# A sparse attention layer on one core: the late query rows are computed in natural order, and the sort of the late half is done a pair later

## The chip, the core and the metric

The kernel runs on one core of a Trainium2 chip. The time is that of one execution in device microseconds. A core has TensorE (PE) for matmuls, VectorE (DVE), ScalarE (ACT), GpSimd (POOL) and SyncE (SP); each works through its own instruction list in order, and SP, ACT and POOL also issue DMAs.

## The reference

`x` has 2708 rows of 1024 numbers, `adj` is a 2708 by 2708 matrix of zeros and ones in which a one stands with probability 0.0014771, so a row has four edges on average.

```python
h = relu(layernorm(x))
q = h @ W_q.T + b_q;  k = h @ W_k.T + b_k;  v = h @ W_v.T + b_v
z = (q @ k.T) / 32 * adj
attn = softmax(where(z == 0, -10000, z), axis=1)
out = x + relu(attn @ v)
```

## The kernel before, in words

**Products.** `W_q` and `W_k` are folded into one matrix M at the start, so that a score is a row of h times M times a row of h. What is called q in the code is h times M, and it is compared with rows of h directly. The result of attention is a weighted sum u of rows of h, and only after that it is multiplied by `W_v`. There are 21 full tiles of 128 rows and one tile of 20 rows. Two tiles at a time (a *unit*) are multiplied by M, and later by `W_v`, with seven block products instead of eight: `blocks` (L646) forms the sums s1 to s4 of the four half rows, `multiply` (L949) issues the seven products (`add_block`, L913, four matmuls of 128x512 each, two passes in the trace). Units 0 to 4 are the q of tiles 0 to 9, tile 10 goes alone at the end of unit 4 (`single_query`, L1131), units 5 to 9 are the q of tiles 11 to 20, units 10 to 19 are the outputs.

**Edges.** Each row of `adj` is searched for its ones: `found` (L330) runs four FIND_INDEX8 on DVE for a tile, `counted` (L324) sums the row on ACT, `listed` (L340) makes up to 16 neighbour numbers of a row, for four tiles at a time.

**Sort.** To gather no more neighbours than needed, the rows are sorted by their number of edges, in two parts: the early part (tiles 0 to 10, `EARLY = 11`) and the late part (the rest). `counts` (L596) makes on DVE a one-hot table `hot` of the counts, `sort` (L613) has two bf16 matmuls on PE (`ps_in` and `ps_all`, L619 and L621) count over it, and seven DVE instructions turn them into the place of each row. `put` (L568) scatters an entry of the table for each row (its neighbours, its number, its count) to DRAM by that place, `reload` (L580) reads the table back in sorted order.

**q and the order of rows.** The early tiles get q in natural order into `q_dram`; attention then gathers a sorted tile's q rows by their number. The late tiles get q in sorted order: their h rows are gathered by the reloaded table (`first_rows`, L556, and `load_rows`, L1095), the result lies in `q_late` in sorted order, and attention reads it with a plain DMA (`fetch`, L760). The rows that sort to the end, the last 20, have no edges and need no q.

**Attention** (`attention`, L859) runs on DVE, ACT and POOL beside the products: for a sorted tile it gathers one row of h for each slot (`fill`, L773), a DVE instruction (L794) multiplies it with q and sums it up to the score, an exponential on ACT and some small DVE instructions make the weights, and DVE sums the weighted rows (L847). `K` says how many slots a sorted tile has.

**What sets the order.** The first stage (until unit 5) has the order of DVE, ACT and POOL written out by hand. `after(i)` (L1162) is called at seven points of each unit n, and `steps_at` (L704) names the search steps at (n, i): `f20` is found and listed for tile 20, `i15` and `j15` are found and listed apart, `p` is counted, `c` is `counts` and `o` is `sort` of the early part, `w` its `put` and `reload`. In unit 3 the late part follows: `counts` at (3, 3), `sort` at (3, 4) with `issue_after`, then `entered` (L632): `put`, `reload`, the rows of units 5 and 6, and the last additions to the sum of all rows (`owe`). `searched` (L712) closes the buffers of the search and opens the gather slots, three of which POOL clears; `ts_of_wv` (L729) makes with 16 DVE instructions (L734 to L737) the sums of `W_v` blocks that SP stores to `tv_dram` (L739). From unit 5 on the scheduler orders POOL and ACT, and `advance` hands out the attention's steps between the products.

Of the kernel before, what the change touches and what calls it, by code (L numbers as in the profile page):

```python
# [18 lines left out]
P = 128  # L19
# [7 lines left out]
TW = 18  # L27
ROWS = 7
HIGH = 11
EMPTY = (10, 20)  # L30
EARLY = 11
# [27 lines left out]
def tile_preln_masked_attention(  # L59
# [76 lines left out]
    nc.vector.memset(zall, 1.0)  # L136
# [10 lines left out]
    rows_i = const.tile([P, NT], I32, name="rows_i")  # L147
    nc.gpsimd.iota(rows_i, pattern=[[P, NT]], base=0, channel_multiplier=1)
    nc.vector.memset(tab, 0.0)
    nc.vector.tensor_copy(tab.bitcast(U32)[:, :, SLOTS:SLOTS + 1], rows_i.unsqueeze(2))  # L150

# [3 lines left out]
    down_i = const.tile([P, ND], I32, name="down_i")  # L155
    nc.gpsimd.iota(down_i, pattern=[[-1, ND]], base=SLOTS, channel_multiplier=0)
    down = const.tile([P, ND], FT, name="down")
# [13 lines left out]
    first_i = const.tile([P, PARTS, 8], I32, name="first_i")  # L171
    nc.gpsimd.iota(first_i, pattern=[[-PW, PARTS], [0, 8]], base=N, channel_multiplier=0)
    first = const.tile([P, PARTS, 8], FT, name="first")
    nc.vector.tensor_copy(first, first_i)

# [17 lines left out]
    def stats(group):  # L193

        G = len(group)
        mv = stat.tile([P, 4, 2], FT, tag="mv", name="mv")
        if tiles[group[-1]][1] < P:
            nc.vector.memset(mv, 1.0)
        xs = []
        for i, t in enumerate(group):  # L200
            t0, n = tiles[t]
            if EARLY + 4 <= t < EARLY + 7:
# [189 lines left out]
    with tc.tile_pool(name="w", bufs=1, side="left") as wp:  # L392
# [136 lines left out]
        follow("f8")  # L529
# [24 lines left out]
    FIRST = EARLY // 2  # L554

    def first_rows(n):  # L556

        rows_of[FIRST + n] = [row_tile(f"qr_{t}") for t in (EARLY + 2 * n, EARLY + 2 * n + 1)]
        for k, row in enumerate(rows_of[FIRST + n]):
            last = gather(row, h_dram[:, :], EARLY + 2 * n + k, SLOTS, P)  # L560
        return last
# [34 lines left out]
    def counts(lo, hi):  # L596


        n = hi - lo
        s1, s2 = [work.tile([P, D], FT, tag="hT", name=name, bufs=2) for name in ("sort", "hot")]  # L600
        sorting[:] = s1, s2
        found = s1[:, 0:n * SLOTS].rearrange("p (t s) -> p t s", s=SLOTS)
        nc.vector.tensor_scalar(found, keys[:, lo:hi], 0.0, None, op0=ALU.is_gt)
        nc.vector.tensor_reduce(bad[:, lo:hi], found, AX.X, ALU.add)
        nc.vector.tensor_copy(tab[:, lo:hi, SLOTS + 1:SLOTS + 2], bad[:, lo:hi].unsqueeze(2))
        nc.vector.tensor_sub(deg[:, lo:hi], bad[:, lo:hi], past[:, lo:hi])
        nc.vector.tensor_scalar_max(deg[:, lo:hi], deg[:, lo:hi], -1.0)
        nc.vector.tensor_tensor(s2.bitcast(BF)[:, 0:ND * n].rearrange("p (d t) -> p d t", d=ND),
                                deg[:, lo:hi].unsqueeze(1).to_broadcast([P, ND, n]),
                                down.unsqueeze(2).to_broadcast([P, ND, n]), op=ALU.is_equal)  # L610
        nc.vector.tensor_scalar(tab.bitcast(U32)[:, lo:hi, 0:SLOTS], keys[:, lo:hi], -1.0, float(N), op0=ALU.mult, op1=ALU.add)

    def sort(lo, hi):  # L613

        s1, s2 = sorting
        W = ND * (hi - lo)
        hot = s2.bitcast(BF)[:, 0:W]
        ps_in = psum.tile([P, NB], FT, tag="tp", name="ps_in")
        nc.tensor.matmul(ps_in[:, :W], before, hot, start=True, stop=True)  # L619
# [3 lines left out]
        nc.vector.tensor_copy(cnt, ps_all[:, :W])  # L623
        run = s1[:, W:2 * W]
        nc.vector.tensor_tensor_scan(run, cnt, cnt, 0.0, op0=ALU.add, op1=ALU.max)
        nc.vector.tensor_sub(run, run, cnt)
        nc.vector.tensor_add(run, run, ps_in[:, :W])
        nc.vector.tensor_mul(run, run, hot)
        nc.vector.tensor_reduce(deg[:, lo:hi], run.rearrange("p (d t) -> p t d", d=ND), AX.X, ALU.add)
        return nc.vector.tensor_copy(pos_i[:, lo:hi], deg[:, lo:hi])  # L630

    def entered():  # L632

        with tc.issue_after(put(EARLY, NT).ins):
            late = reload(EARLY, NT)
        with tc.issue_after(late.ins):
            rows = first_rows(0)
        with tc.issue_after(rows.ins):
            rows = first_rows(1)
        with tc.issue_after(rows.ins):  # L640
            for t in sorted(owed):
                owe(t)
# [42 lines left out]
    def natural_rows(n):  # L685
# [4 lines left out]
    ops_of[0][1]()  # L690
    ops_of[0][2]()
# [20 lines left out]
    def searched():  # L712
        nc.vector.tensor_tensor(bad, bad, total, op=ALU.not_equal)
# [12 lines left out]
        assert len(adj_loads) == NT  # L726
        free.extend([M.rearrange("p i j (a c) w -> p i j a (c w)", a=2)[:, 0, 1, a, :] for a in range(2)] + slots[8:])
# [14 lines left out]

    wanted, g_of, tq, first_q = [], {}, {}, []
# [16 lines left out]
    def fetch(t):  # L760

        assert t in formed
# [3 lines left out]
        if t < EARLY:  # L766
            got = gather(tq[t], q_dram[:, :], t, SLOTS, P)
            if t == order[0]:
                first_q.append(got)
        else:  # L770
            nc.gpsimd.dma_start(tq[t], q_late[(t - EARLY) * P:(t - EARLY + 1) * P, :])

    def fill():  # L773
        while wanted and free:
            t, s = wanted.pop(0)
            g = free.pop(0)
            with tc.issue_after(first_q[0].ins) if first_q else nullcontext():
                gather(g, h_dram[:, :], t, s, P, skip=True)
# [79 lines left out]

    def attention(order):  # L859
# [5 lines left out]
        with tc.issue_after(chain[-1].ins):  # L865
            for lo, hi in parts:
                nc.vector.tensor_scalar(valid[:, lo:hi], ptab.bitcast(U32)[:, lo:hi, 0:SLOTS], float(N) - 0.5, NONE,
                                        op0=ALU.is_lt, op1=ALU.max)
        free.extend(slots[:8])
        fill()  # L870
        yield 0.0
        fetch(order[0])
# [19 lines left out]
    order = [8, 7, 6, 5, 4, 3, 2, 0, 1, 9, 15, 14, 13, 12, 16, 17, 20, 10, 18, 19, 11]  # L892
# [56 lines left out]
    def multiply(n, results, after):  # L949
# [22 lines left out]
        results[3](Y)  # L972
        if n == FIRST - 1:

            single_query()
            opened(n + 1)
        after(6)
# [112 lines left out]
    q_pairs = [(t, t + 1) for t in range(0, EARLY - 1, 2)] + [(t, t + 1) for t in range(EARLY, FULL, 2)]  # L1090
# [4 lines left out]
    def load_rows(unit):  # L1095
        kind, *pair = unit
        rows = []
        for t in pair:
# [4 lines left out]
            if kind == "q":  # L1103
                gather(rows[-1], h_dram[:, :], t, SLOTS, P)
# [19 lines left out]
    def single_turned(s):  # L1124

        if s == 0:
            single["row"] = kept.pop(EARLY - 1)
# [3 lines left out]
    def single_query():  # L1131
# [3 lines left out]
        dst = q_dram[(EARLY - 1) * P:, :]  # L1135
# [8 lines left out]
        ops_of[FIRST][2]()  # L1144
        rows_of.pop(FIRST)
        nc.sync.dma_start(dst[:, lo], q[:, lo])
        formed.add(EARLY - 1)
# [3 lines left out]
    for n, unit in enumerate(units):  # L1151
# [10 lines left out]
        def after(i):  # L1162
            if (n, i) in steps_ahead:
                follow(steps_ahead[n, i])
            if (n, i) == (3, 3):
                counts(EARLY, NT)
            if (n, i) == (3, 4):
                with tc.issue_after(products[-1].ins):
                    placed.append(sort(EARLY, NT))
                entered()  # L1170
            if (n, i) in ((4, 1), (4, 2)):
                ts_of_wv(2 * i - 2, 2 * i)
            if (n, i) == (FIRST - 1, 2):
                next(stream)
# [4 lines left out]
            if (n, i) >= (FIRST, 1):  # L1179
                advance(share)  # L1180
            if nxt is not None:
# [19 lines left out]
                if i == (2 if n == FIRST else 4) and n + 2 >= FIRST and n + 2 < len(units) and n + 2 not in rows_of:  # L1201
# [35 lines left out]
    with tc.issue_after(chain[-1].ins):  # L1237
# [10 lines left out]
        nc.vector.tensor_add(many, many, deg[:, 0:1])  # L1248
    ps_f = psum.tile([P, NB], FT, tag="tp", name="ps_f")
# [210 lines left out]
```

## Time and profile before

| | |
|---|---|
| median of 3 runs | 666.57 us (665.93 to 668.82) |
| the profiled execution | 668.54 us |
| its span, first to last instruction | 666.8 us |
| PE busy, share of the span | 653.1 us, 98% |
| DVE, ACT, POOL busy | 79%, 40%, 60% |
| mean granted TensorE clock | 0.993 |
| matmuls of L913 with x320 and 128x512 outputs | 593 to 598 ns from start to end of one |

The profiled execution is one of its own, 1.97 us above the median; around its span lie 1.7 us. PE's matmuls are pipelined, so they overlap: eight passes of a block take 3.43 us from start to start of the next block. "Idle before" in the profile is the time that an engine waited, with what ended the wait; PEclk is the clock that TensorE was granted, 1.00 being full speed.

### The profile page before, as it was taken

What the parts mean: (1) busy time and instruction counts of PE and PEld (TensorE: products, weight loads), DVE (VectorE), ACT (ScalarE), POOL (GpSimd) and SP (SyncE); (2) the same over time, 40 slices, a digit from 0 to 9 for tenths busy, and PEclk for the clock granted to TensorE, in tenths of its full rate; (3) what the DMA queues carried; (4) which work ended last, traced back from release to release, by engine and by line L of the source; (5) the groups of instructions that cost most, each with busy time, mean ns of one, the idle gap of its engine ahead of it and who ended that gap; (6) DMA issues with size and microseconds to landing.
All of it is one profiled execution on the core that took longest, in us unless ns stands there. A gap on an engine that the chain in (4) does not pass through costs nothing.

```text
span 666.8 us, 6383 instructions
## 1 busy us (share of the span) xinstructions
PE 653.1 (98%) x1770; PEld 333.5 (50%) x1770; DVE 528.1 (79%) x1014; ACT 263.6 (40%) x395; POOL 402.1 (60%) x398
## 2 busy tenths in 40 slices
PE   9999999999998999999999999999999999999994
PEld 5777765444443444444444444444444444445441
DVE  5997899979999404988887999798788998989221
ACT  3558975765843212332241231332332434323200
POOL 2559991666386763775556365574674878863331
PEclk9999999999998999999999999999999999999998
DMA  8995999699757796897889999998987899894631
GB/s 339 407 344 199 375 362 393 222 392 330 256 177 258 276 360 243 283 386 244 308 316 354 375 416 391 308 309 244 339 286 193 236 295 364 232 312 132 149 120 66
DMA packets 62164, 193.24 MB, mean 290 GB/s; under 512 B 9689, under 2 KB 10041, under 8 KB 61226
## 3 DMA queue, kind: packets, MB, share of 16 engines
q0 software_dynamic: 34464, 109.25, 49.8%
q1 hardware_dynamic: 26650, 80.37, 32.4%
q10 hardware_dynamic: 1008, 3.15, 1.3%
q8 instruction: 16, 0.26, 0.1%
q14 instruction: 26, 0.21, 0.1%
HBM read 160.85 MB, written 44.93 MB: 309 GB/s over the span
## 4 chain that ended last, share of the span: by engine, by line
PE 69%; DVE 16%; DMA 6%; POOL 3%; ACT 2%; issue 2%; POOLq 0%; DVEq 0%; ACTq 0%; SPq 0%
PE ps L913 38%; PE psy L913 27%; DMA adj<-in_adj_dram 6%; DVE at L338 6%; PE pt L363 4%; DVE st L216 2%; DVE acc_b L478 2%; POOL hsum L263 1%; DVE s L657 1%; ACT sized L328 1%; DMA bq_sb<-in_bq_dram 1%; DVE wlow L483 1%; ACT x L254 1%; DVE cand L355 1%; DVE wlow L390 1%
## 5 line engine op out<-in xcount | busy, mean ns | idle before, releaser
L549 POOL DMA_INDIRECT g<-h_dram,tab x104 | 125.8, 1210 | 51.5 <-issue 22.7
L913 PE MATMUL psy<-wlow,s 128*128 128x512 f32 x320 | 145.8, 598 | 0.0
L913 PE MATMUL ps<-M,a 128*128 128x512 f32 x320 | 144.1, 593 | 0.1
L794 DVE SCALAR_TENSOR_TENSOR junk<-g,pq 128x1024 uint8<-128x1024 f32 x92 | 112.6, 1224 | 1.9
L847 DVE SCALAR_TENSOR_TENSOR u<-g,coef,u 128x1024 f32<-128x1024 f32 x77 | 98.7, 1282 | 7.8 <-ACT u L839 6.1
L913 PEld LDWEIGHTS psy<-wlow,s 128*128 128x128 f32 x320 | 59.8, 192 | 67.9 <-issue 66.9
L913 PEld LDWEIGHTS ps<-M,a 128*128 128x128 f32 x320 | 59.3, 190 | 68.0 <-issue 67.4
L338 DVE FIND_INDEX8 at<-ones,adj 128x8 uint32<-128x685 f32 (+1 forms) x88 | 74.5, 865 | 0.0
L913 PE MATMUL ps<-wlow,s 128*128 128x512 f32 x160 | 72.0, 592 | 1.3 <-ACT ps L682 1.3
L913 PE MATMUL psy<-wlow,a 128*128 128x512 f32 x160 | 72.0, 593 | 0.3 <-DVE q L994 0.3
L913 PE MATMUL ps<-M,s 128*128 128x512 f32 x160 | 72.0, 592 | 0.0
L328 ACT ACTIVATE sized<-adj 128x2708 uint8<-128x2708 f32 (+1 forms) x22 | 54.3, 2467 | 10.7 <-DMA adj<-in_adj_dram 10.1
L1012 POOL DMA_INDIRECT y<-in_x_dram,tab x19 | 33.9, 1782 | 28.4 <-ACT y L1029 14.0
L913 PEld LDWEIGHTS ps<-wlow,s 128*128 128x128 f32 x160 | 30.3, 190 | 39.9 <-issue 37.3
L913 PEld LDWEIGHTS psy<-wlow,a 128*128 128x128 f32 x160 | 30.3, 190 | 38.9 <-issue 34.0
L913 PEld LDWEIGHTS ps<-M,s 128*128 128x128 f32 x160 | 30.2, 190 | 37.3 <-issue 37.3
L263 POOL TENSOR_TENSOR hsum<-hsum,x 128x1024 f32<-128x1024 f32 (+1 forms) x17 | 40.4, 2374 | 0.4
L657 DVE TENSOR_TENSOR s<-a,pt 128x512 f32<-128x512 f32 x40 | 25.5, 679 | 15.9 <-ACT a L653 15.9
L748 POOL DMA_INDIRECT out_dram<-y,tab x21 | 27.1, 1291 | 15.3 <-DMA y<-in_x_dram,tab 6.9
L653 ACT COPY a<-pt 128x512 f32<-128x512 f32 x60 | 33.2, 593 | 3.7 <-PE pt L363 3.7
L551 POOL DMA_INDIRECT pq<-q_dram,tab x11 | 14.6, 1327 | 31.0 <-DVE junk L794 16.3
L549 POOL DMA_INDIRECT M<-h_dram,tab x20 | 25.4, 1271 | 10.3 <-issue 4.3
(238 smaller groups left out, 892.7 us busy)
## 6 DMA issues: line engine op xcount, KB each, us to landing
adj<-in_adj_dram SPq DMA_DIRECT2D x21, 1354.0 KB, 10.9
x<-in_x_dram SPq DMA_DIRECT2D x21, 512.0 KB, 10.7
h_dram<-x POOLq DMA_DIRECT2D x21, 512.0 KB, 7.1
u_dram<-u POOLq DMA_DIRECT2D x14, 512.0 KB, 6.4
or<-u_dram SPq DMA_DIRECT2D x14, 512.0 KB, 6.7
q_late<-q SPq DMA_DIRECT2D x10, 512.0 KB, 7.9
pq<-q_late POOLq DMA_DIRECT2D x10, 512.0 KB, 6.4
g<-in_wv_dram SPq DMA_DIRECT2D x16, 256.0 KB, 5.3
```

The lines of the kernel that those rows point to most:

```text
L263: nc.gpsimd.tensor_add(hsum[:n], hsum[:n], xt[:n])
L328: nc.scalar.activation(sized[:n], a[:n, :, :PW], AF.Abs, accum_out=total[:n, t:t + 1])
L338: nc.vector.max_index(at[:n, t - first_t, g, :], ones[:n, 0:8], a[:n, g, :])
L363: nc.tensor.transpose(pt[:, c, :], xt[:, k * P:(k + 1) * P], ident)
L549: return nc.gpsimd.indirect_dma_start(out=dst, out_offset=None, in_=src, in_offset=off, bounds_check=N - 1, oob_is_err=False)
L653: nc.scalar.copy(ops[name], bank)
L657: step = (eng or nc.vector).tensor_tensor(ops[name], a, b, op=op)
L748: to = nc.gpsimd.indirect_dma_start(out=out, out_offset=bass.IndirectOffsetOnAxis(ap=ptab.bitcast(U32)[:n, t, SLOTS:SLOTS + 1], axis=0), i ...
L794: chained(lambda: nc.vector.scalar_tensor_tensor(junk, g_of[t][s], 1.0, tq[t], op0=ALU.mult, op1=ALU.mult, accum_out=zall[:, t, s:s + 1]))
L847: chained(lambda: nc.vector.scalar_tensor_tensor(u, g_of[t][s], coef[:, at[t][s]:at[t][s] + 1], u, op0=ALU.mult, op1=ALU.add))
L913: mm = nc.tensor.matmul(bank, a[:, c, :], b[:, c, :], start=False, stop=(c == 3), skip_group_check=True)
L1012: return nc.gpsimd.indirect_dma_start(out=y[:n], out_offset=None, in_=x, in_offset=off, compute_op=ALU.add)
```

## The change

The diff, cut to what the prediction speaks of:

```diff
-EMPTY = (10, 20)
-EARLY = 11
+EMPTY = (9, 20)
+EARLY = 10
+SINGLE = 10
...
-    rows_i = const.tile([P, NT], I32, name="rows_i")
+    rows_i = whole[:, 0:NT]
...
+    query_i = whole[:, 160:160 + NT]
+    for lo, hi in parts:
+        nc.gpsimd.iota(query_i[:, lo:hi], pattern=[[P, hi - lo]], base=0, channel_multiplier=1)
+    nc.vector.tensor_copy(tab.bitcast(U32)[:, :, SLOTS + 2:SLOTS + 3], query_i.unsqueeze(2))
+    HOSTS = FULL - 1 - SINGLE
...
+    nc.gpsimd.iota(place_i[:, 0], pattern=[[1, HOSTS]], base=SINGLE + 1 - EARLY, channel_multiplier=0)
+    nc.gpsimd.iota(place_i[:, 1], pattern=[[0, HOSTS]], base=0, channel_multiplier=1)
...
         ts_of_m(1, 0, 1, 2, 3)
-        follow("f8")
...
     ops_of[0][1]()
+    follow("f8")
     ops_of[0][2]()
...
-    def entered():
-        with tc.issue_after(put(EARLY, NT).ins):
-            late = reload(EARLY, NT)
-        with tc.issue_after(late.ins):
-            rows = first_rows(0)
...
+    def hosted():
+        rank = sorting[0][:, NB:NB + HOSTS]
+        moved = sorting[0][:, NB + HOSTS:NB + 2 * HOSTS]
+        rows = tab.bitcast(U32)[:, SINGLE + 1:FULL, SLOTS]
+        nc.vector.tensor_scalar(rank, deg[:, SINGLE + 1:FULL], start[:, 0:1], None, op0=ALU.subtract)
+        nc.vector.scalar_tensor_tensor(moved, rank, float(FULL * P), rows, op0=ALU.add, op1=ALU.subtract)
+        nc.vector.scalar_tensor_tensor(moved, rank, float(REST) - 0.5, moved, op0=ALU.is_lt, op1=ALU.mult)
+        nc.vector.scalar_tensor_tensor(moved, rank, -0.5, moved, op0=ALU.is_gt, op1=ALU.mult)
+        return nc.vector.tensor_add(whose, moved, rows)
+    def hosts():
+        rank = sorting[0][:, NB:NB + HOSTS]
+        hot = sorting[1].bitcast(BF)[:, 0:HOSTS * REST].rearrange("p (t j) -> p t j", j=REST)
+        nc.vector.tensor_scalar(rank, rank, -1.0, float(SLOTS), op0=ALU.mult, op1=ALU.add)
+        nc.vector.tensor_tensor(hot, rank.unsqueeze(2).to_broadcast([P, HOSTS, REST]),
+                                down.unsqueeze(1).to_broadcast([P, HOSTS, REST]), op=ALU.is_equal)
+        ps = psum.tile([P, NB], FT, tag="tp", name="ps_host")
+        for t in range(HOSTS):
+            nc.tensor.matmul(ps[:REST, 0:2], hot[:, t, :], place_h[:, :, t], start=(t == 0), stop=(t == HOSTS - 1))
...
-                (0, 6): "r6 f13", (1, 1): "f14", (1, 2): "p13 a6", (1, 3): "h6 s8-9 p14", (1, 4): "r8 p15 i15", (1, 5): "j15",
-                (1, 6): "f16 c p16", (2, 1): "f17", (2, 2): "p17 a8", (2, 3): "r10 f18 p18 w h8",
-                (2, 4): "i19 a10", (2, 5): "j19 k10", (2, 6): "f20 f21 p19", (3, 2): "p20", (3, 3): "p21"}
+                (0, 6): "r6 f13", (1, 1): "f14", (1, 2): "p13 a6", (1, 3): "h6 s8-9 p14", (1, 4): "r8 p15", (1, 5): "i15",
+                (1, 6): "j15 c p16", (2, 1): "f16", (2, 2): "f17 p17 a8", (2, 3): "r10 f18 p18 w h8",
+                (2, 4): "a10", (2, 5): "i19 k10", (2, 6): "j19 p19", (3, 1): "f20", (3, 2): "f21 p20", (3, 3): "p21"}
...
-        for i in range(8, HIGH):
-            nc.gpsimd.memset(slots[i], 0.0)
...
-        if t < EARLY:
-            got = gather(tq[t], q_dram[:, :], t, SLOTS, P)
-        else:
-            nc.gpsimd.dma_start(tq[t], q_late[(t - EARLY) * P:(t - EARLY + 1) * P, :])
+        got = gather(tq[t], (q_dram if t < EARLY else q_late)[:, :], t, SLOTS + 2, P)
...
             if kind == "q":
-                gather(rows[-1], h_dram[:, :], t, SLOTS, P)
+                off = bass.IndirectOffsetOnAxis(ap=whose[:, t - SINGLE - 1:t - SINGLE], axis=0)
+                nc.gpsimd.indirect_dma_start(out=rows[-1], out_offset=None, in_=h_dram[:, :], in_offset=off)
...
-            if (n, i) == (3, 3):
-                counts(EARLY, NT)
-            if (n, i) == (3, 4):
-                with tc.issue_after(products[-1].ins):
-                    placed.append(sort(EARLY, NT))
-                entered()
+            if (n, i) == (FIRST - 1, 0):
+                for s in range(8, HIGH):
+                    nc.vector.memset(slots[s], 0.0)
+                next(stream)
+                for t in sorted(owed):
+                    owe(t)
+            if (n, i) == (FIRST - 1, 2):
+                counts(EARLY, NT)
+                nc.vector.tensor_tensor(bad, bad, total, op=ALU.not_equal)
+            if (n, i) == (FIRST - 1, 3):
+                with tc.issue_after(products[-1].ins):
+                    sort(EARLY, NT)
+                placed.append(hosted())
+                for later in (FIRST, FIRST + 1):
+                    rows_of[later] = load_rows(units[later])
+                put(EARLY, EARLY + 6)
+            if (n, i) == (FIRST - 1, 5):
+                hosts()
+            if n == FIRST and 1 <= i <= 3:
+                with tc.issue_after(gathered[-1].ins):
+                    put(EARLY + 2 * i + 4, EARLY + 2 * i + 6)
+            if (n, i) == (FIRST + 1, 0):
+                reload(EARLY, NT)
```

The early part has ten tiles; tile 10 belongs to the late part but still has its q alone at the end of unit 4. Late rows get q in natural order. The 20 rows of the last, short tile have no place among the ten full tiles of units 5 to 9: each of them takes the place of a row without edges (`hosted` makes `whose`, the row of h that each place gets). `hosts` finds with ten small matmuls which place each of the 20 got, and the table carries in a column more where the q of a row lies. Attention gathers the late q by that column. The late `counts` is at (4, 2), the late `sort` at (4, 3). The rows of units 5 and 6 are gathered by `whose` right behind it, without the table, whose entries (`put`) follow in four lots. The one clearing of gather slots goes from POOL to DVE, the search steps from `i15` to `f21` are a step later, and `zall` is cleared after four iotas more have used its memory. The sum over `K` goes from 110 to 111 slots. A final check grows by a term that is above zero if fewer than 20 rows without edges are found there.

More of the change, by code (lines that the diff above doesn't have):

```diff
@@ L154, in tile_preln_masked_attention @@
     ND = SLOTS + 2
-    down_i = const.tile([P, ND], I32, name="down_i")
-    nc.gpsimd.iota(down_i, pattern=[[-1, ND]], base=SLOTS, channel_multiplier=0)
-    down = const.tile([P, ND], FT, name="down")
+    assert ND <= REST
+    down_i = whole[:, 96:96 + REST]
+    nc.gpsimd.iota(down_i, pattern=[[-1, REST]], base=SLOTS, channel_multiplier=0)
+    down = const.tile([P, REST], FT, name="down")
     nc.vector.tensor_copy(down, down_i)
@@ L553, in tile_preln_masked_attention @@
     rows_of = {}
[L554 to L561, printed above, removed]
+    FIRST = SINGLE // 2
     def tiles_of(lo, hi):
@@ L626, in sort @@
         nc.vector.tensor_sub(run, run, cnt)
+        if lo == EARLY:
+            zero = SLOTS * (hi - lo) - lo
+            nc.vector.tensor_copy(start[:, 0:1], run[:, zero + SINGLE + 1:zero + SINGLE + 2])
+            nc.vector.tensor_copy(start[:, 1:2], run[:, zero + FULL:zero + FULL + 1])
         nc.vector.tensor_add(run, run, ps_in[:, :W])
@@ L777, in fill @@
             with tc.issue_after(first_q[0].ins) if first_q else nullcontext():
-                gather(g, h_dram[:, :], t, s, P, skip=True)
+                gathered.append(gather(g, h_dram[:, :], t, s, P, skip=True))
             g_of[t].append(g)
@@ L857, in sums, with marked @@
         done.add(t)
+    def marked(lo, hi):
+        with tc.issue_after(chain[-1].ins):
+            nc.vector.tensor_scalar(valid[:, lo:hi], ptab.bitcast(U32)[:, lo:hi, 0:SLOTS], float(N) - 0.5, NONE,
+                                    op0=ALU.is_lt, op1=ALU.max)
     def attention(order):
@@ L864, in attention @@
         yield 0.0
[L865 to L868, printed above, removed]
+        marked(0, EARLY)
         free.extend(slots[:8])
         fill()
+        fetch(order[0])
         yield 0.0
-        fetch(order[0])
         after = order[1:] + [None, None]
@@ L972, in multiply @@
         results[3](Y)
+        after(6)
         if n == FIRST - 1:
@@ L1087, in of_wv @@
         return wv[j][:, i * 4:(i + 1) * 4, :]
-    q_pairs = [(t, t + 1) for t in range(0, EARLY - 1, 2)] + [(t, t + 1) for t in range(EARLY, FULL, 2)]
+    q_pairs = [(t, t + 1) for t in range(0, SINGLE, 2)] + [(t, t + 1) for t in range(SINGLE + 1, FULL, 2)]
     o_pairs = [(order[i], order[i + 1]) for i in range(0, FULL - 1, 2)]
@@ L1126, in single_turned @@
         if s == 0:
-            single["row"] = kept.pop(EARLY - 1)
+            single["row"] = kept.pop(SINGLE)
         single[s] = small(f"single{s}").rearrange("p (c q) -> p c q", q=P)
@@ L1144, in single_query @@
         ops_of[FIRST][2]()
+        chain.append(behind[-1])
         rows_of.pop(FIRST)
         nc.sync.dma_start(dst[:, lo], q[:, lo])
-        formed.add(EARLY - 1)
+        formed.add(SINGLE)
         banks_of[FIRST] = banks_for(bp_sb)
```

52 lines of the change are left out of this document (30 added, 22 removed).

## The prediction

> **What bounds the kernel now.** I read the page first, then PE's waits, then the chain of waits.
>
> ```profile
> span 666.8 us, 6383 instructions
> PE 653.1 (98%) x1770; PEld 333.5 (50%) x1770; DVE 528.1 (79%) x1014; ACT 263.6 (40%) x395; POOL 402.1 (60%) x398
> PEclk9999999999998999999999999999999999999998
> ```
> ```profile
> PE ps_in L619 <- DVE hot L608: 2.2, 1, 2.2
> PE ps L913 <- ACT ps L682: 1.3, 1, 1.3
> PE psy L913 <- DVE q L994: 0.3, 1, 0.3
> ```
>
> PE is busy for 98% of the span, so the end moves only with PE's instructions, its clock and its waits. Only three waits lie inside the work, and the longest is the late sort's: PE waits for `hot`, a product of DVE. The 13th slice is also the only one before the last with a lower clock. The chain of waits shows that place.
>
> ```profile
> 201.07 3.77 DVE s L657 x3
> ...
> 204.86 0.69 DVE s L657
> ...
> 206.61 0.38 DVE hot L608
> ...
> 207.03 0.26 PE ps_in L619
> ...
> 207.38 5.16 PE psy L913 x8
> ```
> Windows cut at the waits (length, PE busy, clock, DMA share, GB/s):
> ```profile
> 110.30:111.64 1.34, 0.00 (x2) 1.00 1.03 416
> 111.64:115.31 3.67, 3.67 (x9) 1.00 1.01 407
> 204.79:207.03 2.24, 0.01 (x1) 1.00 0.78 258
> 207.38:212.53 5.15, 5.15 (x9) 0.67 0.83 273
> 212.53:215.96 3.43, 3.43 (x10) 1.00 1.04 382
> ```
> PE stood for 2.24 us; the block behind it took 5.15 us instead of 3.43, at a clock of 0.67. The wait therefore cost 2.24 + 1.72 = 3.96 us in this execution. The 1.34 us wait at 110.30 left the clock at 1.00.
>
> **1. The late sort moves from unit 3 to unit 4: -3.96 us.** Its two bf16 matmuls stay, at another place; the wait should not.
>
> ```profile
> 226.98 3.60 PE L913 MATMUL ps<-M,a 128*128 128x512 f32 x8
> 237.28 3.60 PE L913 MATMUL ps<-M,single 128*128 128x512 f32 x8
> 247.58 1.04 PE L363 MATMUL pt<-ident,qr 128*128 128x128 f32 x8
> ```
> ```profile
> 0.97 0.35 DVE L126 MEMSET keys<- 128x352 f32 x1 [0.97 <-PEq L1449]
> ...
> 207.73 0.35 DVE L623 COPY sort<-ps_all 128x198 f32<-128x198 f32 x1
> ...
> 209.92 0.50 DVE L629 TENSOR_REDUCE deg<-sort 128x11 f32<-128x198 f32 x1
> ...
> 213.18 0.68 DVE L734 TENSOR_TENSOR g<-g 128x512 f32<-128x512 f32 x1
> ...
> 223.69 0.69 DVE L737 TENSOR_TENSOR g<-g 128x512 f32<-128x512 f32 x1
> 237.48 0.69 DVE L994 TENSOR_TENSOR q<-psy,p 128x512 f32<-128x512 f32 x1 [2.67 <-PE psy L913]
> ```
> The new place is behind the block that starts at 226.98; four microseconds earlier, that block ends near 226.4. DVE by then has three memsets (352 columns took 0.35, so 1.0 us each), eight sums of `W_v` blocks (16 took 11.2 us, so 5.6) and `counts` as far as `hot` (1.4 us, from the end of the s at 204.86 + 0.69 to 206.99). From 213, when the first sums had their data, that is 213 + 5.6 + 1.4 = 220.0: `hot` is six microseconds early. If that cover goes (the `W_v` loads land late), each microsecond beyond the six is a wait again. What is late next: in unit 3 nothing of DVE stands ahead of PE's block any more, since f21 goes behind the s; these ended at 205.55 before, and the block that reads them began at 215.96, now near 212, so there are six microseconds there too.
>
> **2. PE's 0.3 us wait for L994: -0.3 us.** All search steps from 15 on come one step later, so the search of one tile less lies ahead of that L994, and 0.3 us is all that was missing. A loss is excluded there: DVE's work ahead of it shrinks, and none is added.
>
> **3. The ten host matmuls: +0.7 us.** The trace has none of this form (20 columns of weights, 2 columns moved). The nearest are the small ones:
>
> ```profile
> 105.55 0.28 PE L697 MATMUL ps_b<-part,ones 128*128 128x3 f32 x2
> 105.69 0.86 PE L363 MATMUL pt<-ident,x 128*128 128x128 f32 x6
> ```
> Two passes with three columns kept PE for 0.14 us, so 0.07 each and 0.7 for ten. A gain is excluded, since they are new and PE takes its list in order; the most would be the 0.28 us that one is shown with from start to end, so 2.8. I take 0.7, the pitch in the nearest row. Their weights come from DVE: L994 at 237.48, then an instruction of 0.2 and one like `hot` (0.38), so 1.3 us behind the start of the block at 237.28 plus handover. In the changed order two of that block's four matmuls (1.72 us) stand before them, so no wait, with 0.2 to spare.
>
> **4. The start: +0.3 us.** POOL gets four iotas more ahead of the two bias loads.
>
> ```profile
> 2.85 0.14 POOL L148 IOTA rows_i<- 128x22 int32 x1
> 2.96 0.13 POOL L156 IOTA down_i<- 128x18 int32 x1
> ...
> 4.07 0.58 POOL L394 DMA_DIRECT2D bq_sb<-in_bq_dram  x1
> ```
> ```profile
> 9.37 0.17 DVE L467 TENSOR_SCALAR bq_sb<-bq_sb 128x8 f32<-128x8 f32 x1 [5.70 <-DMA bq_sb<-in_bq_dram]
> ...
> 110.22 0.67 DVE L538 TENSOR_TENSOR bp_sb<-bp_sb 128x512 f32<-128x512 f32 x1
> 110.81 1.28 DVE L657 TENSOR_TENSOR s<-a,pt 128x512 f32<-128x512 f32 x2
> ```
> An iota has a pitch of 0.11 us, so `bq_sb` lands 0.44 us later, DVE starts later, and DVE is what PE waits for at 110.30. With f8 behind bp_sb, ACT's copy no longer ends that wait; the first s does, about 0.1 us before. So +0.44 - 0.1 = +0.3, between 0 (if the `adj` loads on the way absorb it) and +0.44. The other setup copies lie in DVE's 5.70 us of waiting.
>
> **5. Rows without the table: 0.** `whose` is ready after the sort matmuls (226.5), seven sort steps (2.7 us from 207.73 to the end of L629) and about eight small instructions of 0.2 (a 128x8 form took 0.17): 230.8. POOL issues two entries first, so the first rows leave at about 232.5.
>
> ```profile
> 239.56 1.00 POOL L551 DMA_INDIRECT qr<-h_dram,tab  x1 [4.02 <-DMA tab<-tab_dram]
> ```
> ```profile
> DMA to landing us min/median/max: 6.4/7.9/9.2
> ```
> (The second row is that of all gathers of `qr`.) They land by 239 to 242; PE, 3.3 us ahead of 247.58, wants them at 244.3. Before, 239.56 + 6.4 left 1.6 us at most, so there is more room than there was. The wait for the table that goes was hidden, so its removal brings nothing. POOL's ten entries ahead of the first q gather, the late read back and the hsum additions lie under POOL's 40% idle; if not, it is DVE's attention that waits first, and no PE wait after 207 was on it. The inputs have 28 rows without edges between rows 1408 and 2687, counted from the reference's own adjacency, so the 20 find a place and the final check stays at zero.
>
> **6. Late q by gather: 0.** It now needs all late q, while each tile needed one row block before.
>
> ```profile
> 419.45 0.56 POOL L771 DMA_DIRECT2D pq<-q_late  x1 [4.47 <-DVE junk L794]
> ```
> ```profile
> 390.72 3.43 PE psy L913 x8
> ```
> ```profile
> q_late<-q SPq DMA_DIRECT2D x10, 512.0 KB, 7.9
> ```
> The last q block ends at 394.2 and its store lands 7.9 us later, near 403, 16 us ahead of the first read. A gather keeps POOL for 1.00 us (the `qr` row) against 0.56, eleven times, under its idle time. One slot more (two DVE instructions) is within DVE's idle 21%.
>
> **Sum**: -3.96 - 0.3 + 0.7 + 0.3 = -3.26 us. The profiled execution took 668.54, so 665.3. The runs shown are 665.93, 666.57 and 668.82: 668.54 lies beside the longest, 1.97 above the median, which is close to the 1.72 of the lower clock. I take it that the median execution had the wait without the lower clock; it gains 3.26 - 1.72 = 1.54: 665.0. Both ways agree on 665.
>
> The row shows a lower clock behind a gap of 2.24 us. The Trainium skill (TensorE: Matmul & The Clock Gate, "Why this matters for your kernels") asks for gaps above about 3 us before the clock falls, and Part 1 of that page says that the window is free-running. By that rule this gap need not halve the clock in each execution, which agrees with the forecast; the trace has it once.
>
> **The rivals.**
> - *A, the lower clock is in every run of before.* For it: the one trace has it, and only behind the longest wait. Against: the two groups of times. Then 666.57 - 3.26 = 663.3.
> - *B, the change doesn't do what it says: the wait comes back in unit 4*, at `hot` or at the host matmuls. Against: six microseconds of cover at the first. For: the 0.2 us at the second. With 1.5 us of waiting there: 666.5; with the clock down as well 668.
> - *C, slower: the rows of unit 5 come late.* In the changed order a fourth slot gather stands on POOL ahead of the entries and rows; its slot is free only when SP's third `tv_dram` store has landed.
>
> ```profile
> 223.90 12.93 SPq L739 DMA_DIRECT2D tv_dram<-g  x16
> ```
> ```profile
> DMA to landing us min/median/max: 3.7/5.5/8.8
> ```
> (The second row is that of the 16 stores.) SP starts them at 223.90 - 4 = 219.9, the third 1.6 us later, landed at 225.2 to 230.3; the entries want POOL at 229.9. It decides beyond that: with 9 us more, the rows leave at 241.5, land at 249.4, PE waits 5.1 us with the clock down for 1.7 more: 665.0 + 6.8 = 671.8. The longest landing seen, 8.8 us, speaks against it.
>
> **How the numbers follow.** A measurement of this kernel can tell about 0.5% from no change: 3.33 us. Forecast 0.47 (664 to 666), A 0.25, B 0.15, C 0.08, and 0.05 for more gained than I see. Faster than 663.2: half of A, the 0.05 and a little of the forecast's edge, 0.22. Slower than 669.9: C and the worst of B, 0.12. Within: 0.66. The range holds A's lower half and B: 662.4 to 668.0; the host matmuls' upper end (+2.1) and the start's (0 to 0.44) lie in it.
>
> **What would show it.** No wait of PE for `hot` of the sort, which stands in unit 4, and the clock at full speed in the 13th and 14th slices (step 1); no wait for L994 (2); ten matmuls in 0.7 us with no DVE wait (3); DVE's L467 at 9.8 and PE's stop at 110.3 longer by 0.3 (4); `qr` issued near 232 and no PE wait at `pt` (5); no DVE wait at the first late `pq` (6). A PE wait of over 1 us past 200 would prove me wrong, as would before's runs that all have the lower clock.

## The result and the profile after

The changed kernel takes 665.14 us (median of 15 executions, 664.93 to 665.28), the kernel before took 668.81 beside it (median of 15, 665.38 to 671.6). The medians lie 3.67 us apart. The ratio is 0.9952, with a 95% interval of 0.9936 to 0.9968 that excludes 1: a gain, of about the 0.5% that I had said could just be told from no change. The profiled execution of the changed kernel took 665.11, against 668.54 before: 3.43 less. The forecast of 665.0 holds. What it took the median of before to be does not: with 15 executions instead of 3 that median is 2.2 us higher. One execution of before, beside a_again, took 3925.8 us; it counts in the median of 668.74 in the table below (668.68 without it) and in nothing else.

The page of the changed kernel (first lines and the row of the granted clock), then PE's waits:

```profile
span 663.3 us, 6435 instructions
...
PE 651.6 (98%) x1780; PEld 333.4 (50%) x1780; DVE 537.2 (81%) x1036; ACT 264.9 (40%) x395; POOL 404.5 (61%) x400
...
PEclk9999999999999999999999999999999999999998
```
```profile
PE ps L940 <- DVE s L685: 1.4, 1, 1.4
PE ps_y L473 <- POOL hsum L108: 1.2, 1, 1.2
PE ps_z L438 <- DVE wlow L499: 0.4, 1, 0.4
```

The wait for `hot` (2.2) and the one for L994 (0.3) are gone, the clock row has no dip before the last slice, and PE is busy for 1.5 us less although it got ten instructions more. The wait near 110 is now put down to the first s (DVE's sums of half rows, from `blocks`) instead of ACT's copy, and is 0.1 longer. The chain of waits through the new place of the sort (start, length, instruction):

```profile
226.21 0.09 PE ps_in L627
226.31 0.09 PE ps_all L629
226.40 3.45 PE ps L940 x8
...
235.00 0.34 PE ps_host L664 x10
...
244.12 0.87 PE pt L379 x8
```

PE goes through the sort without a stop. The ten host matmuls cost 0.34 us. DVE's part (timeline: start, length, instruction, and in brackets its idle time before):

```profile
9.77 0.17 DVE L483 TENSOR_SCALAR bq_sb<-bq_sb 128x8 f32<-128x8 f32 x1 [5.38 <-DMA bq_sb<-in_bq_dram]
```
```profile
186.55 0.68 DVE L1021 TENSOR_TENSOR q<-psy,p 128x512 f32<-128x512 f32 x1
```
```profile
220.47 0.38 DVE L616 TENSOR_TENSOR hot<-deg,down 128x216 bf16<-128x216 f32 x1
```

DVE starts 0.40 later than before (9.37). `hot` is ready at 220.85, 5.4 us ahead of PE. The second row is the L994 of before (L1021 here); PE no longer waits for it. Windows of the changed kernel (length, PE, PEld, DVE, ACT, POOL busy, clock, DMA share, GB/s): the wait near 110, and the block that in before came behind the sort:

```profile
110.70:112.12 1.42, 0.01 (x1) 0.03 (x1) 1.42 (x3) 0.96 (x4) 0.00 (x0) 1.00 1.04 419
...
204.74:208.17 3.43, 3.43 (x9) 1.52 (x9) 3.43 (x9) 0.68 (x2) 2.12 (x2) 1.00 0.29 59
```

The block takes 3.43 at a clock of 1.00; before it took 5.15 at 0.67.

### The profile page after: what moved, and what is told of

It is laid out like the page before. It is cut to its first block, busy times and chain, and to the rows that moved or that the text cites. A ratio compares the mean times of both kernels' runs of the same rounds, so it can differ in the third digit from the quotient of the medians.

```text
span 663.3 us, 6435 instructions
## 1 busy us (share of the span) xinstructions
PE 651.6 (98%) x1780; PEld 333.4 (50%) x1780; DVE 537.2 (81%) x1036; ACT 264.9 (40%) x395; POOL 404.5 (61%) x400
## 4 chain that ended last, share of the span: by engine, by line
PE 92%; DVE 4%; DMA 1%; issue 1%; POOL 1%; POOLq 0%; DVEq 0%
PE ps L940 45%; PE psy L940 31%; PE ps_y L438 6%; PE pt L379 5%; PE ps_z L438 4%; DVE acc_b L494 2%; DMA bq_sb<-in_bq_dram 1%; DVE wlow L499 1%; DVE at L354 1%; DVE wlow L501 0%; PE ps_h L1146 0%; PE ps_v L549 0%; DVE t L496 0%; DVE wlow L406 0%; DVE wlow L500 0%
## 5 line engine op out<-in xcount | busy, mean ns | idle before, releaser
L564 POOL DMA_INDIRECT g<-h_dram,tab x105 | 124.2, 1182 | 78.7 <-issue 21.3
L940 PE MATMUL psy<-wlow,s 128*128 128x512 f32 x320 | 144.1, 592 | 0.0
L871 DVE SCALAR_TENSOR_TENSOR u<-g,coef,u 128x1024 f32<-128x1024 f32 x78 | 100.1, 1283 | 6.9 <-ACT u L863 5.0
L775 POOL DMA_INDIRECT out_dram<-y,tab x21 | 25.7, 1224 | 15.4 <-DMA y<-in_x_dram,tab 7.1
L953 ACT COPY psy<-ps 128x512 f32<-128x512 f32 x20 | 11.4, 572 | 46.8 <-PE ps L940 42.1
```

What stands on the lines that cost most here:

```text
L564: return nc.gpsimd.indirect_dma_start(out=dst, out_offset=None, in_=src, in_offset=off, bounds_check=N - 1, oob_is_err=False)
L775: to = nc.gpsimd.indirect_dma_start(out=out, out_offset=bass.IndirectOffsetOnAxis(ap=ptab.bitcast(U32)[:n, t, SLOTS:SLOTS + 1], axis=0), i ...
L871: chained(lambda: nc.vector.scalar_tensor_tensor(u, g_of[t][s], coef[:, at[t][s]:at[t][s] + 1], u, op0=ALU.mult, op1=ALU.add))
L940: mm = nc.tensor.matmul(bank, a[:, c, :], b[:, c, :], start=False, stop=(c == 3), skip_group_check=True)
```

## The experiments

All times are medians; "before" is the kernel before, run beside each group on the same chip.

| kernel | us (range, executions) | before beside it | ratio to before (95%) |
|---|---|---|---|
| b_again | 669.84 (666.85 to 671.48, 12) | 669.93 | 0.9990 (0.9968 to 1.0012) |
| b_counts | 668.95 (665.41 to 670.40, 12) | 669.93 | 0.9980 (0.9956 to 1.0005) |
| b_noadd | 665.46 (664.47 to 671.33, 12) | 669.93 | 0.9954 (0.9926 to 0.9983) |
| a_back | 671.25 (667.42 to 676.87, 12) | 669.93 | 1.0031 (1.0000 to 1.0061) |
| b_f8 | 670.32 (666.46 to 673.32, 12) | 671.60 | 0.9982 (0.9960 to 1.0004) |
| b_iota | 671.67 (668.77 to 672.59, 12) | 671.60 | 1.0002 (0.9986 to 1.0017) |
| a_start | 680.43 (679.84 to 681.33, 5) | 671.60 | 1.0134 (1.0106 to 1.0162) |
| a_f8 | 681.71 (681.61 to 682.10, 4) | 671.60 | 1.0156 (1.0124 to 1.0189) |
| a_again | 665.01 (664.89 to 665.10, 12) | 668.74 | 0.9959 (0.9943 to 0.9976) |
| a_start2 | 664.13 (664.09 to 669.80, 10) | 668.74 | 0.9937 (0.9915 to 0.9959) |
| b_best | 666.49 (663.91 to 671.47, 12) | 668.74 | 0.9979 (0.9953 to 1.0005) |
| a_best | 662.82 (662.78 to 663.39, 6) | 668.97 | 0.9907 (0.9890 to 0.9924) |

**b_again: what differs between executions of before.** No edit.

> The kernel before, unchanged, to see how its executions differ. Theory: the wait for hot is set by where POOL's addition to hsum (2.37 us at 201.90 in the trace of before, started behind a DMA landing) falls beside DVE's s (2.56 us for the one at 202.27, 0.69 for the one at 204.86). So the wait differs from execution to execution, by up to 2.56 - 0.69 = 1.87 us, and the lower clock (1.72 us) comes with the longer waits: times between 668.5 - 1.87 - 1.72 = 665.0 and some us more, with span and mean clock going together. Rival: the wait is always 2.24 us and only the lower clock comes and goes: two groups, 1.7 us apart.

The profile taken this time is another one than that in the prediction. PE's waits and two windows:

```profile
PE ps L913 <- ACT ps L682: 4.3, 1, 4.3
...
PE ps_in L619 <- DVE hot L608: 0.9, 1, 0.9
```
```profile
115.12:121.86 6.74, 6.74 (x9) 2.88 (x10) 6.64 (x12) 2.90 (x4) 0.00 (x0) 0.54 0.58 193
121.86:125.30 3.44, 3.44 (x10) 1.53 (x9) 3.37 (x11) 3.04 (x3) 1.31 (x4) 1.00 0.35 138
```

The wait for `hot` is 0.86 instead of 2.24, with no dip behind it, as the theory has it. In this trace POOL's addition ran at 204.26, ahead of the s that it stretched in the trace of before, and that s takes 0.69:

```profile
208.75 0.69 DVE L657 TENSOR_TENSOR s<-s,a 128x512 f32<-128x512 f32 x1
```

But the wait near 110 has grown from 1.34 to 4.29, and the clock falls behind that one, for twice as long: the block takes 6.74 us, where it took 3.67 in before. Neither theory had this. Two things add up in it. The first is `adj`. ACT's row for one tile in the trace of before, then in this one:

```profile
76.67 2.47 ACT L328 ACTIVATE sized<-adj 128x2708 uint8<-128x2708 f32 x1 [0.99 <-DMA adj<-in_adj_dram]
```
```profile
79.28 2.47 ACT L328 ACTIVATE sized<-adj 128x2708 uint8<-128x2708 f32 x1 [3.06 <-DMA adj<-in_adj_dram]
```

The load landed 2.6 us later. The windows from 70 to 76 show the DMA, before first:

```profile
70.00:76.00 6.00, 6.00 (x16) 4.38 (x15) 5.76 (x15) 5.68 (x5) 5.75 (x7) 1.00 0.98 356
```
```profile
70.00:76.00 6.00, 6.00 (x15) 4.38 (x14) 5.83 (x13) 6.00 (x7) 5.81 (x7) 1.00 0.85 284
```

The same instructions, 284 GB/s instead of 356: a slower spell of transfers, whose cause no trace shows. DVE's search of the last tile of that batch starts 1.96 us later for it (95.63 against 93.67). The second is POOL again. DVE's `cand` behind that search (the first step of `listed`), in before, then here, and POOL's addition beside it here:

```profile
97.17 1.00 DVE L350 TENSOR_TENSOR cand<-first,at 128x128 f32<-128x128 f32 x1
```
```profile
99.13 2.52 DVE L350 TENSOR_TENSOR cand<-first,at 128x128 f32<-128x128 f32 x1
```
```profile
99.10 2.39 POOL L263 TENSOR_TENSOR hsum<-hsum,x 20x1024 f32<-20x1024 f32 x1
```

The late load brought `cand` under a whole addition, and it took 1.52 longer. 1.96 + 1.52 are the 3.5 us that DVE is late by 104, and they make 3 us more of PE's wait. In the trace of b_f8 the load is 1.52 late as well, but `cand` falls into the gap between two additions and takes 0.29; there PE's wait is only 1.58:

```profile
98.69 0.29 DVE L350 TENSOR_TENSOR cand<-first,at 128x128 f32<-128x128 f32 x1
```

So before has two waits that come and go, POOL's additions are in both, and each had its own dip of the clock in a trace. Where I write "the late `adj`" below, both parts are meant. The theory also had time and clock go together, which not every execution does: one of 669.88 has a mean clock of 0.997, as high as the shortest beside it (665.25). What made it long no trace shows.

**b_noadd: what makes the wait for `hot`.**

```
-            if add:
+            if add and t != 9:
                 nc.gpsimd.tensor_add(hsum[:n], hsum[:n], xt[:n])
-            else:
+            elif not add:
                 owed[t] = xt
```


> Before without one instruction: POOL's addition of tile 9 to hsum (the one at 201.90) is left out, so tile 9's rows are missing in the sum that rows without edges take. Theory (that addition is what stretches DVE's s and so makes most of the wait): the s takes 0.69 instead of 2.56, the wait falls from 2.24 to about 0.4, the clock stays full: 668.5 - 1.87 - 1.72 = 665.0. Rival (the s is slow for another reason, or the order on DVE alone makes the wait): wait 2.2, 668.5.

The trace of before has POOL's addition and DVE's s side by side (POOL's timeline, then DVE's):

```profile
201.90 2.37 POOL L263 TENSOR_TENSOR hsum<-hsum,x 128x1024 f32<-128x1024 f32 x1
```
```profile
202.27 2.56 DVE L657 TENSOR_TENSOR s<-s,a 128x512 f32<-128x512 f32 x1
204.86 0.69 DVE L657 TENSOR_TENSOR s<-a,s 128x512 f32<-128x512 f32 x1
```

The s begins inside the addition and ends 0.56 behind its end (204.27); the next one of the same shape takes 0.69. Without the addition, in b_noadd:

```profile
205.01 0.69 DVE L657 TENSOR_TENSOR s<-s,a 128x512 f32<-128x512 f32 x1
```

Seven of the twelve executions take 664.47 to 665.66, about the 665.0 that the theory gives; the other five, 669.1 to 671.3, among them the profiled one, whose trace has the late `adj` and a wait of 4.2. That trace has no wait for `hot`; b_again's, with about the same wait near 110, had 0.86. So one POOL instruction that PE never waits for made most of the wait for `hot`: it held DVE. The edit takes away this one addition; those near 99 stay, and so do long executions. The Trainium skill (SBUF — State Buffer, "SBUF: two separate sides") says that DVE and GpSimd share one pair of ports by an exclusive lock, for the whole instruction, where DVE has two SBUF inputs or runs in a mode that takes two ports. The rows agree: this s has two inputs from SBUF, and the first two s, one of whose inputs comes from PSUM, took 1.28 for both although they ran into the addition as well.

**b_counts: take the wait away by order alone.**

```
-            if (n, i) == (3, 3):
+            if (n, i) == (3, 2):
                 counts(EARLY, NT)
```


> Before with one thing moved: the eight instructions of counts stand ahead of the four s of unit 3 on DVE instead of behind them; every other engine's list is as before. Theory (the gain of the change is the wait for hot and the clock behind it): hot is ready near 201.1 + 1.5 = 202.6, ahead of PE's 204.8; no wait, full clock, 668.5 - 3.96 = 664.6, with executions within 0.5 us of each other. The s end near 207.1 and are wanted at 212. Rival (the gain comes from the rows without the table, the natural order or the other moves): it stays near 668.5.

The wait for `hot` is gone from the trace, the gain is not there: 668.95. The trace that was taken has the late `adj` (a wait of 4.3 near 110). And the order only changed which instruction POOL holds, now the first of `counts`, 0.25 us long in before (DVE's row, then POOL's):

```profile
204.04 3.38 DVE L603 TENSOR_SCALAR sort<-keys 128x176 f32<-128x176 f32 x1
```
```profile
203.77 1.14 POOL L584 DMA_DIRECT2D tab<-tab_dram  x1 [1.16 <-DMA tab_dram<-tab,pos_i]
204.92 2.37 POOL L263 TENSOR_TENSOR hsum<-hsum,x 128x1024 f32<-128x1024 f32 x1
```

It ends 0.13 behind the addition, but it stood from 0.88 ahead of the addition's row, while POOL issued a load. Such an issue alone held nothing in b_noadd, where the s of 0.69 at 205.01 lies inside the one from 204.29 to 205.43. Why the hold begins ahead of the row stays open.

My 664.6 was wrong: counted on one trace, it held neither for the other wait nor for the neighbour on POOL. How the two waits share the median, no trace here says.

**a_back: put the sort back.** The changed kernel with `counts` at (3, 3), `sort` and `hosted` at (3, 4) and the old search steps. The expectation has the rows' gathers move too; in the edit the rows of units 5 and 6 are still gathered in unit 4.

> The changed kernel with the late sort put back into unit 3 (counts behind its s, the two sort matmuls and the rows' gathers behind them) and the search steps f16 to f21, i15, j15, i19, j19 at their old places; natural order, rows without the table and host matmuls stay. Theory (the move of the sort is the gain): PE waits for hot again by about 2.2 us with a lower clock behind it, and 0.3 for q: 665.1 + 2.24 + 1.72 + 0.3 = 669.4, with executions apart by some us. Rival (something else of the change is the gain): 665.1.

```profile
PE ps_in L627 <- DVE hot L616: 4.7, 1, 4.7
```
```profile
209.60:217.50 7.90, 7.90 (x15) 3.61 (x16) 6.13 (x19) 0.00 (x0) 3.80 (x4) 0.70 1.00 349
217.50:221.00 3.50, 3.50 (x9) 1.52 (x8) 3.12 (x5) 0.57 (x1) 3.01 (x2) 1.00 1.06 394
```

The wait is back, larger than in before, with the lower clock behind it, and so is the spread, 667.4 to 676.9. Against before on the same chip the ratio is 1.0031, where the changed kernel's is 0.9952; against the changed kernel (665.01 and 665.14, on other chips) it is 6.1 to 6.2 us. That is more than the gain, since `hot` comes later here than in before. So the test shows that the place of the late sort, with the search steps that move with it, decides between gain and none; which of the two does how much it does not show.

**b_f8 and b_iota: is it the start, or f8?** Before with f8 between `ops_of[0][1]()` and `ops_of[0][2]()`; before with this ahead of `rows_i`:

```
+    for lo, hi in ((0, EARLY), (EARLY, NT), (0, EARLY), (EARLY, NT)):
+        nc.gpsimd.iota(rows_i[:, lo:hi], pattern=[[P, hi - lo]], base=0, channel_multiplier=1)
```


> Before with f8 alone at the change's place. If f8's place decides the long wait at 110: no execution with it, times between 664.6 and 668.5 (the wait for hot stays). If not: as before, 665 to 672 with a median near 669.

> Before with four iotas of 11 columns more on POOL at the start, three iotas more than before ahead of bq_sb's load, so that DVE starts about 0.3 us later. Theory: the same spread as before, median near 669 to 670. Rival (the later start is what keeps the adj loads from being late): few or no executions with the long wait at 110, times of 665 to 668.8, median near 667.

Both spread as before and have its median within the interval: neither edit alone is the gain. The profile of b_f8 has a wait of 5.2 for `hot`, that of b_iota one of 2.6. Neither shows the long wait near 110 (b_f8 has the late load, but not the hold of `cand`), so they do not settle what keeps it away.

**a_start and a_f8: the start priced, and a surprise.**

```
+    nc.gpsimd.dma_start(bk_sb, bk)
+    nc.gpsimd.dma_start(bq_sb, bq)
     rows_i = whole[:, 0:NT]
...
-        nc.gpsimd.dma_start(bk_sb, bk)
-        nc.gpsimd.dma_start(bq_sb, bq)
```
a_f8 has `follow("f8")` back behind the last `ts_of_m(1, ...)`.

> The changed kernel with POOL's two bias loads issued ahead of the iotas instead of behind them. Step 4 of the prediction: bq_sb lands about 0.7 us earlier than in the changed kernel, DVE starts earlier, PE's wait near 110.7 shrinks by that: 665.1 - 0.4 to - 0.7 = 664.4 to 664.7. Rival for the spread of before (adj loads that land late near 75 to 95 us make PE wait 4.3 us instead of 1.4 at 110, in some executions of before and in none of the changed kernel's): if it is the later start that keeps the changed kernel out of it, some executions here take 668 to 670.

> The changed kernel with the search of tile 8 (f8) back at its old place, ahead of the subtraction in bp_sb, so that ACT's copy of bp_sb is what PE waits for near 110. Prediction's step 4: 0.1 us longer, 665.2, all executions alike. Rival: the new place of f8 is what keeps the changed kernel's executions alike; then some here take 668 to 670.

Both took 680 to 682, which no theory had. PE's waits of a_start, then ACT's:

```profile
PE pt L381 <- ACT a L681: 8.1, 1, 8.1
PE ps L940 <- ACT ps L710: 4.5, 1, 4.5
```
```profile
ACT a L681 <- remote: 19.7, 3, 10.1
```

In unit 5, between 241 and 261, ACT stands for 10.1 and 9.2 us before copies of transposes that PE had finished 6 us and more before, released by something that the trace does not name; PE then stands for 8.1 and 4.5 us. The instruction lists of a_start and of the changed kernel differ in the place of the two loads alone. So the runs were taken again elsewhere.

**a_again and a_start2: the kernel or the place?** No new edit.

> The changed kernel, unchanged, once more beside before. Theory: the time is the kernel's own: 665, within 0.5 us, wherever it runs. Rival (what made a_start and a_f8 take 680, ACT's copies of unit 5 standing 7 to 19 us behind finished transposes between 244 and 266, is a state that the changed kernel can also fall into): 680, or two groups.

> The same kernel as a_start (bias loads ahead of the iotas), again, beside the changed kernel. If the 680 us belong to this instruction order: 680 again while a_again is at 665. If they belong to the place where it ran: the time of a_again less 0.4 to 0.7.

On this other chip the changed kernel takes 665.01, all within 0.2 us, and a_start2 takes 664.13: the 680 us do not belong to the instruction order alone. What held ACT there stays open, and so does whether the changed kernel would show it on that chip: it did not run there. a_f8 is inconclusive. Beside a_again the bias loads ahead of the iotas are worth 0.88 us. `bq_sb` is there 0.58 earlier than in the changed kernel (9.77):

```profile
9.19 0.17 DVE L483 TENSOR_SCALAR bq_sb<-bq_sb 128x8 f32<-128x8 f32 x1 [3.46 <-DMA bq_sb<-in_bq_dram]
```

One of the ten took 669.80, and that is the profiled one, with a wait near 110 of 3.5 us: 2.04 more than the 1.42 of the changed kernel, 0.95 by the load (94.88 against 93.93) and 1.09 by `cand` (2.31 against 1.22). So the changed kernel's family is not free of it: none in 27 executions of the changed kernel itself, one in ten here.

**b_best: both waits taken out of before.** b_counts, and `follow("f8")` behind `ts_of_m(0, 1, 3, 2)`.

> Before with two moves on DVE and none elsewhere: counts ahead of the s of unit 3 (as in b_counts), and f8 behind the first s and the three T blocks instead of ahead of bp_sb. Theory: no wait for hot (-2.24, and -1.72 for the clock), and no wait of 1.34 at 110, since bp_sb and the s come 3.4 us earlier: 668.5 - 3.96 - 1.34 = 663.2; where the adj loads land late by 3.5 us the wait at 110 is then 1 us instead of 4.3 and the clock stays full: 664 to 664.5. Rival (the long wait is not f8 and the late loads): as b_counts, 665.4 to 670.

```profile
PE ps_in L618 <- DVE hot L607: 0.8, 1, 0.8
PE pt L363 <- DMA qr<-h_dram,tab: 0.4, 1, 0.4
PE psy L913 <- DVE q L994: 0.4, 1, 0.4
```
```profile
200.34 3.13 DVE L602 TENSOR_SCALAR sort<-keys 128x176 f32<-128x176 f32 x1
```

The wait near 110 is gone and the best execution takes 663.91, but the median is 666.49 and the spread stays. POOL's addition again holds the first of `counts`, and once PE is early, the rows of unit 5, which here come through the table, are late. What its longer executions wait for was not profiled. By these two moves on DVE alone, before does not get to 665.

**a_best: the changed kernel with both moves.** a_start, and f8 behind the T blocks:

```
-    follow("f8")
     ops_of[0][2]()
     banks_of = {0: banks_for(bp_sb)}
     ts_of_m(0, 1, 3, 2)
+    follow("f8")
```


> a_start (the changed kernel with the bias loads ahead of the iotas) with f8 behind the first s and the three T blocks on DVE, so that the s come 3.4 us earlier. Theory: the wait near 110.7, 1.42 us in the changed kernel and about 0.5 in most executions of a_start, goes, also where the adj loads land late (then 3.46 in a_start, now about 0.1): 664.1 - 0.5 = 663.6, all executions within 0.5 us. Rival (what f8 is moved past, the T blocks and the small products behind them, is late next): 664 to 665. Rival (the 680 us of a_start's first place): 680 again.

PE's only wait in the trace, and PE's rows around 110:

```profile
PE ps_y L473 <- POOL hsum L108: 1.2, 1, 1.2
```
```profile
107.03 3.70 PE L940 MATMUL ps<-M,a 128*128 128x512 f32 x8
110.57 3.60 PE L940 MATMUL ps<-wlow,s 128*128 128x512 f32 x8
```

662.82, 6.1 us below before beside it and 2.2 below a_again (another chip): faster than both kernels. The wait near 110 is gone. The first s now ends at 108.1, some 2.4 us before PE wants it (an estimate from the rows), so a delay like the 2.04 of a_start2 would just fit; whether any of the six executions had one is not known, so this is not shown. The forecast 663.6 was 0.8 too high: the usual wait that it took as 0.5 is 1.1 in the trace of a_start, and 664.13 less 662.82 makes 1.3.

## Why the prediction was right, and where it was not

- **Step 1, the late sort (-3.96): right.** The wait and the dip are gone; `hot` is ready at 220.85 (220.0 was said), PE comes at 226.2, and a_back brings wait, dip and spread back. The chain that was given for the wait (s, then `counts`, then `hot`) was true but not the cause of its size: the s row with 3.77 us for three was read as work, and 1.87 us of it was POOL's addition. In the changed kernel that collision is still there (an s of 3.71 us at 201.26), and nobody waits for it: there are 5.4 us of cover.
- **Step 2, L994 (-0.3): right.** No such wait after.
- **Step 3, host matmuls (+0.7): the size was off.** They took 0.34, 0.034 each, half of the pitch that was taken from matmuls of three columns. No DVE wait, as said: their weights were ready 0.4 ahead (234.60 against 235.00). The 1.3 us of that sum should read 1.5 (0.20 + 0.69 + 0.2 + 0.38), which fits the 0.2 to spare.
- **Step 4, the start (+0.3): a little low.** DVE starts 0.40 later (0.44 was said) and PE leaves the stop near 110 at 112.12 instead of 111.64: 0.48. The early waits differ by some tenths between executions. All of the iotas ahead of the loads together are worth 0.88 (a_start2 against a_again), of which `bq_sb` shows 0.58.
- **Steps 5 and 6 (0): right in the time, too little in the words.** `qr` is issued at 233.2 and PE does not wait for it; no late q was waited for. "Its removal brings nothing" holds against before. But with PE only 3.3 us earlier at that place (244.25 against 247.58), b_best already waits for rows that come through the table, from a sort 20 us earlier than the changed kernel's. That rows without the table are what lets the sort go a unit later was not tried by itself; it is argued from these two times.
- **The sum.** -3.26 was forecast for the profiled execution, -3.43 came. With the measured terms it is -3.96 - 0.3 + 0.34 + 0.48 = -3.44, so the mechanism accounts for all of it, and the two mis-sized terms nearly cancel.
- **The step that failed is the median of before.** "The median execution had the wait without the lower clock" was built on three numbers, of which the profile showed one. The runs show other things in its place: the wait for `hot` itself varies (0.9, 2.2 and 2.6 in three traces of the same DVE order), and the wait near 110 grows from 1.3 to 4.3 where `adj` lands late and `cand` meets POOL's addition, which my trace did not have. With 15 executions the median is 668.81, close to the profiled one, so the profiled sum was the one to trust. Both ways gave 665 because the second took a median 2.2 too low and corrected it by just the difference. That the second way met the time is luck: it forecast a gain of 1.54 between the medians, and 3.67 came.
- **Rivals.** A (663.3) did not come: the lower clock is in many executions of before, but 665.38 shows that not in all. B did not come: PE passes the host matmuls without a wait. C did not come: the fourth slot gather did stand ahead of the rows, at 229.29, and was issued in time. What no rival had is the effect on the spread: 6.2 us of range before, 0.35 after.
- **The clock.** The Trainium skill's threshold (TensorE: Matmul & The Clock Gate, "Why this matters for your kernels": gaps above about 3 us) was weighed as a reason to doubt the dip. The measurement decides against that use: in the traces 2.24 and 2.60 us of standing were each followed by a dip, 1.3 to 1.6 us in seven traces never, 3.5 to 5.2 us in six traces by a dip of double length. The long executions at full clock (669.88 in b_again, 669.50 in b_noadd, both 0.997) leave open whether that is so each time.

What stays open: why `adj` lands late in many executions of before and why none of the 27 of the changed kernel has the long wait near 110; how much of the gain in the median is this wait and how much the one for `hot`; and what held ACT in a_start and a_f8, and whether the changed kernel would be slower than before on that chip.

## What to carry to other kernels

When a DVE row of one shape shows two durations, look at POOL's timeline at the same microsecond before you count the longer one as work; a POOL instruction off the path can be most of a wait on it, and a late load can bring a DVE instruction under one. Take a wait out by giving its producer some microseconds of cover, and not by a new order that only moves the collision to the next instruction. And when executions of a kernel spread by several microseconds, profile it twice before you say what the median contains.

## What the runs showed of the hardware that I had not expected

- The dip of the clock came in two lengths behind the waits for `hot` and near 110. Behind 2.24 us the block took 5.15 instead of 3.43 at a mean clock of 0.67, that is 3.4 us at half; behind 4.29 us it took 6.74 instead of 3.67 at 0.54, and the dip had begun in the wait (0.92 over those 4.29 us). That wait cost PE 7.4 us in all.
- The same DVE instruction (128x176) took 0.25, 3.13 and 3.38 us, the longer ones until 0.1 us behind POOL's addition of 2.37 us and from some tenths ahead of its row; `cand` (128x128) took 0.29, 1.00 and 2.52.
- Ten matmuls of 128x20 weights and two columns, back to back, took 0.34 us.
- The DMA engines moved 284 and 356 GB/s in the same six microseconds of two executions of one kernel.
